# VectorE's own sums in the first slot of three, and the background matmuls off the slots of the groups of 6

## The chip, the cores and the metric

The kernel runs on one core of one Trainium2 chip. The metric is the time of one execution on the device in microseconds (us); less is better. The engines are called PE (TensorE), DVE (VectorE), ACT (ScalarE), POOL (GpSimd) and SP (SyncE, which issues the DMAs), as in the profile.

## The reference

Input is x of shape (8, 128, 36, 36) in float32: 8 images, 128 channels, 1296 positions. Cut to what matters:

```python
x = x + conv_attention(group_norm(x))          # 3x3 convolutions to q, k, v; softmax attention
t = tokens(x)                                  # (8, 1296, 128)
h = layer_norm(t)
q = h @ Wq.T + bq;  k = h @ Wk.T + bk
scores = einsum('bijd,d->bij', tanh(q[:, :, None] + k[:, None]), w) + bw
t = t + softmax(scores) @ h                    # additive attention over all pairs of tokens
t = t + expert_ffn(layer_norm(t))              # 64 experts, each takes the 8 best tokens
```

The third part is by far the largest: for each of 8 x 1296 x 1296 pairs of tokens it wants the sum of 128 values w[d] tanh(q[i,d] + k[j,d]).

## The kernel before, in words

**The loop over pairs.** The tanh's are not computed one by one. Signed sums of groups of 5 or of 6 of the channels give exponentials of queries and keys (qf and kf), and for each group two products over 32 or 64 rows: a numerator n and a denominator d. The score is the sum over all groups of n/d. The division is made by ACT as exp(-ln d), called lq.

A **unit** is one image b (8), one chunk c of 432 queries (3), and one tile j of 128 keys (10, and an eleventh, the "remainder" tile of 16 keys). A full unit has NP = 12 **slots**, numbered k = 0 to 11. They come in triples: k % 3 = 0 and 1 are two slots of the groups of 5 (each with two products on 32 rows, and the rows alternate between the upper and the lower half), k % 3 = 2 is a slot of the groups of 6 (two products on 64 rows). In this text slots 0, 1 and 2 mean the place in a triple. A remainder unit has 2 slots with another layout (`REM_SLOTS`). In all there are 240 full and 24 remainder units.

In slot p of the loop the engines are given, in this order:

1. `take_turns(p, k)`: background steps that move a result out of PSUM (on DVE or ACT);
2. `numerators(p)`: two matmuls n, each into a bank of its own (L949);
3. `denominators(p + LAG)`: two matmuls d for the slot three later (L949), ACT's Ln of them (L972), and in every odd slot the Exp over two slots (L975);
4. `terms(p, ns)`: DVE multiplies n by lq. In most slots the products go into a tile rp (L1003) and POOL adds them up in accp (L1010, L1012). In the slots of `DVE_PAIRS` DVE also adds: it multiplies in place in PSUM (L997) and adds both banks to its own sum accd (L999); in the first of these slots it writes accd at once (L992, then L993, L994);
5. `matmul_turn(p, k)`: matmuls of one background step.

After the last slot of a unit POOL adds the two halves of accp and accd (L1019, L1021), and seven slots later ACT makes e = exp(score) of it (L1032). For a remainder unit matmuls (L1045, rem) add up rp instead.

**Background.** While one image is in the loop, the normalization, convolutions (pc), first attention (s, pa0), tokens and keys (pk) of the next image, the query blocks of the next chunk (pq), the weighting with e (pa1) and the gates of the image before run as generators in four lanes: `first_of_all`, `urgent`, `gates`, `background`. Each generator says whether its next step wants matmuls or takes a result. A slot gives matmuls to one step at most. Only `first_of_all` may run in every slot; the others are kept out of `take_turns` in the slots of `DVE_PAIRS`, and out of `matmul_turn` in the slot just before one of these, or when a balance of columns (`PACE` = 400 more per slot) is below zero:

```python
def take_turns(p, k):
    for lane in lanes:
        if lane.due(p, False) and (k not in DVE_PAIRS or lane is first_of_all):
            lane.run(p)
```

**PSUM.** Of the 8 banks, 4 are two pairs for d (`ps_d`, each pair freed by ACT's Ln), and 4 (`ps_n`) go in turn to n (two a slot) and to every background result (one a step).

**Order.** Nothing is reordered later (`manual_schedule`): each engine runs its instructions in the order in which the loop gives them, and waits where a buffer or an operand isn't there.

Of the kernel before, what the change touches and what calls it, by code (L numbers as in the profile page):

```python
# [54 lines left out]
NP = len(SLOTS)  # L55
IN_TURN = [m + i for m in range(NF // 2) for i in (0, NF // 2)]
LAG = 3
SHIFT = 6.5
DVE_PAIRS = (2, 5, 8, 11)
PACE = 400  # L60


# [8 lines left out]
def kernel(  # L71
# [58 lines left out]
    with ExitStack() as loop, ExitStack() as score:  # L130
# [277 lines left out]
        def conv_keys(b):  # L408
            k = convolved["k"] = big_tile("k0")
            if b == 0:  # L410
                taps["k"] = load_taps("wk_t")
            for r0, nr in KROWS:
                yield from conv_turns(
                    taps["k"], (r0, nr), 1, grid(k[:, r0 * WV : (r0 + nr) * WV], WV), True
                )
# [251 lines left out]
        def keys(b, tiles):  # L667

            xT = prepared[b][1]
            yield matmuls(1)  # L670
            for t in tiles:
                o, n = KT[t]
                first = (b, t) == (0, order[0])
                if first:
                    kf_of[0] = kfp.tile([128, NF, 128], F32, tag="kf", name="kf")
                for q0 in (0, NF // 2):
                    some = slice(q0, q0 + NF // 2)
                    pk = aux("pk1").rearrange("p (q t) -> p q t", t=128)
                    for q in range(NF // 2):
                        bmm(pk[:, q, :n], a_k[:, (q0 + q) * 128 : (q0 + q + 1) * 128],  # L680
                           xT[:, o : o + n], start=True, stop=True)
                    yield TAKE
                    if first:
                        ks = kf_of[0][:, some, :]
                    else:
                        ks = kstp.tile([128, NF // 2, 128], F32, tag="ks", name="ks")
                    nc.scalar.activation(ks[:, :, :n], pk[:, :, :n], AF.Exp)
                    kd3 = kd[b][t].rearrange("p (q t) -> p q t", t=128)[:, some, :]
                    if n == REM:

                        for x in range(2):
                            nc.gpsimd.tensor_scalar(
                                ks[:, :, (x + 1) * n : (x + 2) * n], ks[:, :, :n],
                                pairs[:, min(q0, 1), x : x + 1], None, ALU.mult,
                            )
                        nc.sync.dma_start(kd3[:, :, : 2 * n], ks[:, :, n : 3 * n])
                    else:
                        nc.sync.dma_start(kd3, ks)
                    if q0 > 0:
                        made.add((b, t))  # L700
                    yield matmuls()
# [85 lines left out]
        def gating(b):  # L787
            yield from gate_logits(b, range(NCH))
            yield from gate_tokens(b)
# [114 lines left out]
        def residuals(n):  # L904

            for b in range(n):
                res.append(big_tile("res")[:, :N])
                nc.sync.dma_start(res[b], t2d[b])
                yield step()
# [11 lines left out]
        slots = []  # L921
# [4 lines left out]
        def prefetch(u):  # L926
            if u < len(units) and u not in kf_of:
                b, c, j = units[u]
                assert (b, j) in made
                n = 128 if j < NKT - 1 else 32  # L930
                kf = kfp.tile([128, NF, 128], F32, tag="kf", name="kf")
                nc.sync.dma_start(
                    kf[:, :, :n], kd[b][j].rearrange("p (q t) -> p q t", t=128)[:, :, :n]
                )
                kf_of[u] = kf

        def new_block(b, c, q):
            qf = qfp.tile([128, 2, CH], F32, tag="qf", name="qf")
            qf_of[b, c, q] = qf
            return query_block(b, c, q, qf)  # L940
# [36 lines left out]
        def numerators(p):  # L977
            ns = [ps_n.tile([128, 512], F32, tag="n", name="n") for _ in range(banks(*slots[p]))]
            products(*slots[p], 1, ns)
            return [ps[:, :CH] for ps in ns]  # L980

        def terms(p, ns):

            u, k = slots[p]
            lq = lq_of[u, k // 2]
            o = 2 * (k % 2)
            mult = nc.vector.tensor_mul
            rem = units[u][2] == NKT - 1
            if k in DVE_PAIRS and not rem:
                if k == DVE_PAIRS[0]:  # L990
                    live["d"] = acc.tile([128, CH], F32, tag="accd", name="accd")
                    mult(live["d"], ns[0], lq[:, o, :])  # L992
                    mult(ns[1], ns[1], lq[:, o + 1, :])  # L993
                    nc.vector.tensor_add(live["d"], ns[1], live["d"])  # L994
                else:
                    for h in range(2):
                        mult(ns[h], ns[h], lq[:, o + h, :])  # L997
                    for h in range(2):
                        nc.vector.tensor_add(live["d"], ns[h], live["d"])  # L999
            else:  # L1000
                rp = rpp.tile([128, 2, CH], F32, tag="rp", name="rp")
                for h, n in enumerate(ns):
                    mult(rp[:, h, :], n, lq[:, o + h, :])  # L1003
                if rem:
                    live.setdefault("rem", []).extend(rp[:, h, :] for h in range(len(ns)))
                elif k == 0:
                    live["r"] = rp
                elif k == 1:
                    live["p"] = acc.tile([128, 2, CH], F32, tag="accp", name="accp")
                    nc.gpsimd.tensor_add(live["p"], live["r"], rp)  # L1010
                else:
                    nc.gpsimd.tensor_add(live["p"], live["p"], rp)  # L1012
            if k % 2 == 1:
                lq_of.pop((u, k // 2))
# [53 lines left out]
        balance = [0]  # L1068
# [3 lines left out]
# [5 lines that stand above are left out]
        def matmul_turn(p, k):  # L1077


            before = behind[0]  # L1080
            for lane in lanes:
                while lane.due(p, True) and behind[0] == before:
                    paced = balance[0] < 0 or k + 1 in DVE_PAIRS
                    if lane is not first_of_all and paced or lane is gates and urgent:
                        break
                    lane.run(p)
            balance[0] = min(balance[0] - (behind[0] - before) + PACE, 2 * PACE)
# [25 lines left out]
        for p, (u, k) in enumerate(slots):  # L1113
            b, c, j = units[u]
            rem = j == NKT - 1
            if k == 0:
                prefetch(u + 2)
                if c == 0 and j == 1:
                    if b > 0:
                        gates.append(gating(b - 1))  # L1120
                    if b == NB - 1:
                        gates.append(residuals(4))
                    if b + 1 < NB:
                        background.extend(
                            (normal(b + 1), conv_keys(b + 1), layer0(b + 1), tokens(b + 1),
                             keys(b + 1, range(NKT)))
                        )
            take_turns(p, k)
            ns = numerators(p)
            denominators(p + LAG)  # L1130
            terms(p, ns)
            if pending and pending[0][0] <= p:
                exps(p, *pending.popleft()[1:])
            last = p + 1 == len(slots) or slots[p + 1][0] != u

            if j == order[-1] and u + 1 < len(units) and k % 3:
                used = IN_TURN.index(SLOTS[k][0]) + 1
                if used < NF:
                    first_of_all.append(new_block(*units[u + 1][:2], IN_TURN[used]))
            elif j == order[-2] and last and u + 2 < len(units):  # L1140
                first_of_all.append(new_block(*units[u + 2][:2], IN_TURN[0]))
            matmul_turn(p, k)
            if last and rem:
                first_of_all.append(rem_scores(p, u, live.pop("rem")))
            elif last:
                pending.append((p + 7, u, sums(u)))
        while pending:
            exps(p, *pending.popleft()[1:])
        take_turns(len(slots), 0)
        assert not first_of_all and not gates and not background  # L1150
        score.close()

# [205 lines left out]
```

The softmax here doesn't subtract the row's maximum and nothing guards it: scores larger than these inputs give would overflow.

## Time and profile before

| | |
|---|---|
| median of 3 runs | 6138.88 us (6137.63 to 6139.3) |
| the profiled execution | 6140.74 us |
| its span, first to last instruction | 6139.0 us |
| granted TensorE clock | 0.985 |
| busy: PE, ACT, DVE, POOL | 5957.9, 5279.9, 4796.4, 4597.7 us |
| n matmuls (L949) | 11520 records, 3325.3 us busy |
| d matmuls (L949) | 11520 records, 2991.6 us busy |
| ACT Ln (L972), one | 0.878 us, 2928 times |
| ACT Exp (L975), one | 1.638 us, 1464 times |
| DVE product into rp (L1003), one | 0.600 us, 3912 times |
| DVE product in place (L997), one | 0.608 us, 1440 times |
| DVE sum (L999), one | 0.602 us, 1440 times |
| POOL sum (L1012), one | 2.025 us, 1440 times |

Busy time is the time in which at least one instruction of the engine, or of the group, ran. Each matmul of float32 has two records, so the 11520 records of n are 2 products in 2880 slots. Matmuls on different rows overlap, so the groups of PE add up to more than PE's own busy time. "<-" in brackets names what the instruction, or the weight load before it, had waited for.

### The profile page before, as it was taken

The numbers are of one execution on the slowest core, as the hardware profiler recorded it, in microseconds if no ns is written. First come the engines' busy times: TensorE is split into PE (matmuls) and PEld (weight loads), VectorE is DVE, ScalarE is ACT, GpSimd is POOL, SyncE is SP. The second block draws the span as 40 slices with busy tenths as digits, with TensorE's granted clock in tenths as the row PEclk, the third lists the DMA queues.
The fourth block names the chain that finished last, engine by engine and source line by source line (L and its number), as shares of the span: only waits on it lengthen the run. The fifth ranks groups of instructions, "written<-read, shape, count | busy, mean of one in ns | idle before, by whom it ended". The sixth has DMA issues, their size and how long they took to land.

```text
span 6139.0 us, 93072 instructions
## 1 busy us (share of the span) xinstructions
PE 5957.9 (97%) x33480; PEld 2862.1 (47%) x33480; DVE 4796.4 (78%) x9521; ACT 5279.9 (86%) x5371; POOL 4597.7 (75%) x2819
## 2 busy tenths in 40 slices
PE   7999999999999999999999999999999999999996
PEld 5454444544544445444455444454444544544443
DVE  4787878877788787877888777887778877788882
ACT  1888898888988888889998889888898888999990
POOL 4777777777787777778778786877777777787870
PEclk9999999999999999999999999999999999999997
DMA  1210011100110002100111001110011100110008
GB/s 44 70 37 22 25 62 38 34 25 28 68 43 20 26 27 71 39 24 23 44 55 39 22 24 59 44 39 22 20 65 40 34 25 28 58 50 29 28 20 297
DMA packets 151519, 270.87 MB, mean 44 GB/s; under 512 B 45648, under 2 KB 76752, under 8 KB 151056
## 3 DMA queue, kind: packets, MB, share of 16 engines
q1 hardware_dynamic: 151056, 264.92, 13.0%
q8 instruction: 264, 4.33, 0.3%
q14 instruction: 199, 1.63, 0.1%
HBM read 200.41 MB, written 64.19 MB: 43 GB/s over the span
## 4 chain that ended last, share of the span: by engine, by line
PE 77%; ACT 7%; DVE 6%; issue 6%; POOL 2%; DMA 1%; SPq 0%; DVEq 0%; POOLq 0%; ACTq 0%
PE n L949 37%; PE d L949 12%; PE pa L284 7%; PE pc L284 5%; ACT lq L972 5%; PE s L284 3%; PE pk L284 3%; PE pq L284 3%; DVE rp L1003 2%; DVE n L997 1%; DVE accd L999 1%; PE d L954 1%; ACT lq L975 1%; DMA w<-in_weight_dram 1%; PE n L954 1%
## 5 line engine op out<-in xcount | busy, mean ns | idle before, releaser
L1012 POOL TENSOR_TENSOR accp<-accp,rp 128x864 f32<-128x864 f32 x1440 | 2915.8, 2025 | 1041.0 <-DVE rp L1003 948.8
L949 PE MATMUL n<-qf,kf 32*128 32x432 f32 (+1 forms) x11520 | 3325.3, 574 | 46.5 <-ACT e L1032 13.3
L949 PE MATMUL d<-qf,kf 32*128 32x432 f32 (+1 forms) x11520 | 2991.6, 561 | 38.7 <-ACT lq L972 38.2
L972 ACT ACTIVATE lq<-d 128x864 f32<-128x864 f32 x2928 | 2524.2, 878 | 542.6 <-PE d L949 512.1
L1003 DVE TENSOR_TENSOR rp<-n,lq 128x432 f32<-128x432 f32 x3912 | 2173.3, 600 | 743.5 <-PE d L949 542.8
L975 ACT ACTIVATE lq<-lq 128x1728 f32<-128x1728 f32 (+1 forms) x1464 | 2398.2, 1638 | 46.3
L949 PEld LDWEIGHTS n<-qf,kf 32*128 32x128 f32 (+1 forms) x11520 | 1206.4, 184 | 1600.3 <-DVE rp L1003 581.5
L949 PEld LDWEIGHTS d<-qf,kf 32*128 32x128 f32 (+1 forms) x11520 | 1090.0, 185 | 422.1 <-issue 224.7
L997 DVE TENSOR_TENSOR n<-n,lq 128x432 f32<-128x432 f32 x1440 | 814.9, 608 | 142.1 <-PE n L949 88.5
L999 DVE TENSOR_TENSOR accd<-n,accd 128x432 f32<-128x432 f32 x1440 | 866.3, 602 | 24.6
L1010 POOL TENSOR_TENSOR accp<-rp 128x864 f32<-128x864 f32 x240 | 485.2, 2022 | 197.7 <-DVE rp L1003 195.6
L711 POOL TENSOR_SCALAR qf<-qf,cs_s 128x432 f32<-128x432 f32 x192 | 260.9, 1365 | 45.0 <-ACT qf L710 44.4
L284 PEld LDWEIGHTS pa<-xh,e 128*108 128x108 f32 x1920 | 222.5, 174 | 131.1 <-DVE rp L1003 56.0
L1021 POOL TENSOR_TENSOR accd<-accp,accd 128x432 f32<-128x432 f32 x240 | 265.2, 1105 | 18.8
L1019 POOL TENSOR_TENSOR accp<-accp 128x432 f32<-128x432 f32 x240 | 264.4, 1102 | 16.7
L284 PE MATMUL pa<-xh,e 128*108 128x129 f32 x1920 | 262.9, 283 | 8.7 <-ACT e L1032 5.2
L284 PE MATMUL s<-q,k 128*116 128x432 f32 x480 | 230.3, 568 | 1.7 <-DVE q L316 1.4
L284 PEld LDWEIGHTS pk<-xT,a_k 128*128 128x128 f32 x1408 | 171.2, 192 | 107.0 <-DVE n L997 33.7
L462 POOL TENSOR_TENSOR tot<-tot,e 116x432 f32<-116x432 f32 x192 | 212.0, 1104 | 6.0 <-ACT e L471 4.6
L471 ACT ACTIVATE e<-s 116x432 f32<-116x432 f32 x240 | 124.9, 520 | 98.3 <-PE s L284 97.9
L284 PE MATMUL pa<-e,vw 116*128 116x432 f32 x480 | 204.6, 549 | 0.0
L284 PE MATMUL pk<-xT,a_k 128*128 128x128 f32 (+1 forms) x1408 | 202.5, 287 | 0.1
(213 smaller groups left out, 3788.4 us busy)
## 6 DMA issues: line engine op xcount, KB each, us to landing
kf<-kd SPq DMA_DIRECT2D x239, 512.0 KB
kd<-ks SPq DMA_DIRECT2D x158, 256.0 KB
w<-in_weight_dram SPq DMA_DIRECT2D x32, 1024.0 KB
wk_t<-wk_t_d SPq DMA_DIRECT2D x7, 768.0 KB
wv_t<-wv_t_d SPq DMA_DIRECT2D x7, 768.0 KB
wq_t<-wq_t_d SPq DMA_DIRECT2D x7, 768.0 KB
x<-in_x_dram SPq DMA_DIRECT2D x8, 648.0 KB
t<-tokd SPq DMA_DIRECT2D x96, 54.0 KB
```

The lines of the kernel that those rows point to most:

```text
L284: mm(out, lhsT, rhs, **kw)
L711: nc.gpsimd.tensor_scalar(qf[:, 1, :], qf[:, 0, :], cs_s[:, q : q + 1], None, ALU.mult)
L949: mm(outs[h][:, :CH], kf[rows[h], q, :], qf_of[b, c, q][rows[h], part, :], start=True, stop=True)
L972: nc.scalar.activation(lq[:, o : o + n, :], d[:, :n, :CH], AF.Ln)
L975: nc.scalar.activation(some, some, AF.Exp, scale=-1.0)
L997: mult(ns[h], ns[h], lq[:, o + h, :])
L999: nc.vector.tensor_add(live["d"], ns[h], live["d"])
L1003: mult(rp[:, h, :], n, lq[:, o + h, :])
L1010: nc.gpsimd.tensor_add(live["p"], live["r"], rp)
L1012: nc.gpsimd.tensor_add(live["p"], live["p"], rp)
L1019: nc.gpsimd.tensor_add(s[:, 0, :], s[:, 0, :], s[:, 1, :])
L1021: nc.gpsimd.tensor_add(d, s[:, 0, :], d)
```

## The change

`DVE_PAIRS`, the slots in which DVE adds, goes from k = 2, 5, 8, 11 (the slots of the groups of 6) to k = 0, 3, 6, 9 (the first slot of each triple). The rules that refer to it move along: background results are now taken in slots 1 and 2 of a triple rather than 0 and 1. Background matmuls, kept out of the slot before, are now behind slots 0 and 1 rather than behind slots 2 and 0. A "% NP" makes this rule hold over the end of a unit. The first two rp tiles of a unit are those of k = 1 and 2 rather than 0 and 1. `place` keeps the two slots of a remainder unit as they were: the first may have background matmuls behind it, the second may not, and both may take.

```diff
-DVE_PAIRS = (2, 5, 8, 11)
+DVE_PAIRS = (0, 3, 6, 9)
...
-                elif k == 0:
+                elif k == 1:
                     live["r"] = rp
-                elif k == 1:
+                elif k == 2:
                     live["p"] = acc.tile([128, 2, CH], F32, tag="accp", name="accp")
                     nc.gpsimd.tensor_add(live["p"], live["r"], rp)
...
-                    paced = balance[0] < 0 or k + 1 in DVE_PAIRS
+                    paced = balance[0] < 0 or (k + 1) % NP in DVE_PAIRS
...
-            take_turns(p, k)
+            place = (1, NP - 1)[k] if rem else k
+            take_turns(p, place)
...
-            matmul_turn(p, k)
+            matmul_turn(p, place)
...
-        take_turns(len(slots), 0)
+        take_turns(len(slots), 1)
```

## The prediction

> **What bounds the kernel now.** I read part 1 of the page first, then the chain of waits, the timeline of one stretch, and last the table of waits.
>
> ```profile
> PE 5957.9 (97%) x33480; PEld 2862.1 (47%) x33480; DVE 4796.4 (78%) x9521; ACT 5279.9 (86%) x5371; POOL 4597.7 (75%) x2819
> PE 77%; ACT 7%; DVE 6%; issue 6%; POOL 2%; DMA 1%; SPq 0%; DVEq 0%; POOLq 0%; ACTq 0%
> ```
>
> TensorE (PE) carries 77% of the chain that ended last, but ScalarE (ACT, 86%) is not far behind: where little background work is about, ACT sets the pace. A busy PE is also no proof of work, since a matmul that waits in the middle of a pair shows its neighbour as busy. So I looked at single slots. The timeline at 2016 us shows a whole triple of slots with convolution work (pc) behind slots 0 and 2:
>
> ```profile
> 2016.32 0.63 PE L949 MATMUL n<-qf,kf 32*128 32x432 f32 x2
> 2016.34 0.63 PE L949 MATMUL d<-qf,kf 32*128 32x432 f32 x2
> ...
> 2017.26 1.36 PE L284 MATMUL pc<-xwin,wq_t 128*128 128x216 f32 x6
> 2017.35 1.12 DVE L1003 TENSOR_TENSOR rp<-n,lq 128x432 f32<-128x432 f32 x2 [0.25 <-PE d L949]
> ...
> 2018.55 0.63 PE L949 MATMUL n<-qf,kf 32*128 32x432 f32 x2
> ...
> 2019.49 1.00 PE L949 MATMUL n<-qf,kf 64*128 64x432 f32 x4
> ...
> 2020.32 0.89 PE L949 MATMUL d<-qf,kf 64*128 64x432 f32 x4
> ...
> 2020.72 1.12 DVE L997 TENSOR_TENSOR n<-n,lq 128x432 f32<-128x432 f32 x2
> ...
> 2021.14 1.03 PEld L284 LDWEIGHTS pc<-xwin,wq_t 128*128 128x128 f32 x6 [0.62 <-DVE rp L1003]
> ...
> 2021.75 1.24 DVE L999 TENSOR_TENSOR accd<-n,accd 128x432 f32<-128x432 f32 x2
> ...
> 2022.43 0.19 PEld L949 LDWEIGHTS n<-qf,kf 32*128 32x128 f32 x2 [0.27 <-DVE accd L999]
> ```
>
> The reader is to see three things. In a slot of 5 (32 rows) n and d start together on different rows and both are over in 2017.26 - 2016.32 = 0.94 us. In a slot of 6 (64 rows) d follows n: 2021.14 - 2019.49 = 1.65 us. And VectorE's own sums (L997, L999) stand in the slot of 6; the next n starts just as the first L999 ends. The triple takes 6.11 us.
>
> I measured every slot of the loop in the trace's records, from its first n matmul to that of the next slot: slots 0, 1, 2 of a triple take 1.89, 1.31 and 2.76 us in the mean (5.95 a triple; 960 triples and the 48 slots of the remainder tiles make the loop's 5825 us). The shortest slot with the same work behind it is 0.84 us for a bare slot of 5 and 1.65 for a bare slot of 6; with pc behind 2.14 and 2.85, with s 1.85 and 2.56, with pk 1.93 and 2.74, with pa x4 2.59 and 3.30. Summed over all slots these shortest lengths make 4969 us, so 854 us are waits: 261 in slots 0, 319 in slots 1, 274 in slots 2. The table of waits says on what:
>
> ```profile
> PEld n L949 <- DVE rp L1003: 581.5, 1032, 1.5
> PEld n L949 <- DVE accd L999: 198.5, 472, 1.6
> PEld d L949 <- ACT lq L972: 146.1, 199, 5.0
> ```
>
> (columns: total us, times, longest; about 0.27 us of each is the weight load's usual distance.) n waits for a PSUM bank that VectorE has to free.
>
> **What the Trainium skill says.** *TensorE: Matmul & The Clock Gate*, section "The mechanism", says that matmuls on different row groups overlap while matmuls stay in program order; the trace agrees (four matmuls in 0.94 us at 2016.32). So a blocked n holds up d and the background matmul behind it. *Perfetto Trace Analysis*, "Optimization Strategy", says that the same gap repeating on the engine that should be saturated can mean too few SBUF or PSUM buffers; the L949 waits above fit that.
>
> **The change part by part.** The counts of all instructions stay the same. What moves is which slot VectorE's four-step sums and the background matmuls stand in.
>
> *The rotation of banks.* n and the background results take turns in the four ps_n banks A to D, so every fourth taker gets the same bank. Before, with work behind slots 2 and 0: slot 2 takes B, C, its background D, the next slot 0 takes A, B. That slot's second n needs B, free after the first L999 of slot 2. PE's cover between the two n is 1.65 + background, 2.56 us with s, 2.85 with pc. After, with work behind slots 0 and 1: slot 0 takes A, B, background C, slot 1 takes D, A. Its second n needs A, free after the first L999 of slot 0. The cover is now 0.84 + background: 1.85 with s or pq, 1.93 with pk, 2.14 with pc, 2.59 with pa x4.
>
> *What has to be covered.* From the start of n to the start of the first product is 1.10 us (5th percentile in all kinds of slots; 1.03 in the stretch shown). From there to the end of the first L999 is 1.63 us (5th percentile 1.62, median 1.63 of 720). Sum 2.72; with about 0.06 to the matmul, 2.78. The second n stands 0.11 behind the first. So the stall is 2.78 - 0.11 - cover: 0.82 us with s or pq, 0.74 with pk, 0.53 with pc, 0.08 with pa x4. In the first triple of a unit L992 frees A after one step (1.10 + 0.60), and no stall is left: it applies to three triples in four. With nothing behind slot 0 the wait moves to the next taker of A and is up to 1.1 us, mostly where ACT sets the pace anyway.
>
> *Sum on PE.* 674 of 960 slots 0 have background behind them now; three quarters of these by a mean of 0.5 us over the mix (an estimate from the four stalls above) is **+253 us**. Background behind a slot of 5 costs PE 0.09 us more than behind a slot of 6 (1.85 - 0.84 against 2.56 - 1.65 with s, the same with pc and pa, none with pk); some 640 move: **+55 us**. Queued behind a stalled n are d, and so ACT's Ln of it, and the background matmul.
>
> *What comes back.* The waits of before do not all stay. Slot 2 no longer takes a bank that an eviction issued one slot earlier must free (n needed C one bare slot after background 0; now a slot with background lies between), and stalls give ACT time to catch up. Per unit of 12 slots the floor rises from 20.3 to 20.5, with the stalls 22.8 us, against ACT's 21.6 busy and 23.8 measured now. In 86 of 239 units the new PE path alone is longer than the whole unit now, 95 us in sum; in the rest the stall replaces waits in part. I take back 130 of the 308: **+170 us net**, my choice between 95 and 308. After the remainder tiles the first rp of a unit now comes in slot 1 rather than 0, so that VectorE's wait for rem (1.97 against 1.63 us for such a slot 1, 24 times) goes: -8 us, in the rounding.
>
> *Costed at nothing.* GpSimd's additions: rp is made in slots 1 and 2 rather than 0 and 1, and after the last slot come one addition of 2.02 and two of 1.10 us; e is wanted seven slots (14 us) later. SyncE's DMAs (kd, kf, tokd) move by one slot, and kf is fetched two units (48 us) ahead. Each background step still meets two matmul slots and two eviction slots in three; the pace of 400 a slot is unchanged. Query blocks keep slots 1 and 2. If one of these covers failed, L1012's buffer (rp) would be late next.
>
> The profiled execution is 6140.7 us (span 6139.0), 1.9 above the median 6138.9; from the median, 6139 + 170 = **6310 us**.
>
> **The rivals.**
> *ACT hides it.* Where ACT is at 6.0 of 6.35 us (triples with pk) or 5.7 of 6.2 (s), PE's stall may fall into time that PE waits now. For it: 854 us of waits. Against: with pc ACT has 5.2 of 6.11 and PE runs without pause, so about 126 triples pay 0.3 to 0.4 us whatever happens. Net -50 to +90 us: 6090 to 6230, likely 6180.
> *Faster.* Slots of 2.1, 2.1, 1.65 us on PE are more even than 2.1, 0.9, 2.85, and evictions get a slot more. If all 274 us of waits in slots 2 vanish and the four-step sums are in time, -274 + 55 = -219: 5920. It decides from where 0.84 + background reaches 2.67 us; only pa comes close, so I expect a part of it at most (-30 to -220).
> *d comes in bursts.* d of slot 2 and of the next slot 0 now follow within 1 us, after a gap of up to 3 us; ACT idles in the gap and is late after it. With two d banks this would add 0.2 us to most triples on top: 6310 + 150 = 6460.
> That the code does not do what it says is excluded by the order of instructions of the changed program: L997 stands in slots 3, 6, 9 and pc behind slots 0 and 1.
>
> **How the numbers follow.** Stall as summed, 0.52; hidden by ACT 0.20 (of which faster 0.02, same 0.05, slower 0.13); faster by evenness 0.15; bursts 0.13. Cases of more than 0.2% (12 us, about what a measurement of this kernel can tell from no change): faster 0.17, same 0.05, slower 0.78. The range 6080 to 6470 takes in hidden, summed and bursts; the main case alone is 6200 to 6400.
>
> **What would show it.** "PEld n <- DVE accd L999" grows from 198 us to above 400; slots 1 (or 0 to 1 together) grow by about 0.5 us and slots 2 shrink to near 1.65 to 1.8; "PEld n <- DVE rp L1003" falls; ACT's share falls to about 84%. Wrong if L999 waits do not grow, or if slot 2 loses more than slots 0 and 1 gain.

## The result, and the profile after

The changed kernel takes 6349.24 us (median of 4 runs, 6345.87 to 6351.59) against 6139.09 us for the kernel before: ratio 1.0343, 95% interval 1.033 to 1.0356, so 210 us slower. The profiled execution takes 6351.6 us, its span is 6349.9 us.

Part 1 of the page after (busy us, share of the span) and the engine line of part 4, the chain that ended last:

```profile
PE 6059.6 (95%) x33480; PEld 2874.2 (45%) x33480; DVE 4809.4 (76%) x9521; ACT 5305.9 (84%) x5371; POOL 4599.7 (72%) x2819
PE 82%; DVE 10%; ACT 3%; issue 3%; POOL 2%; DMA 1%; SPq 0%; POOLq 0%; DVEq 0%; ACTq 0%
```

No engine has more to do: the counts are the same, and DVE, ACT and POOL are busy for nearly as long as before. But DVE's part of the chain has gone from 6 to 10%. The table of waits after (who waited for whom: total us, times, longest us):

```profile
PEld n L949 <- DVE rp L1003: 498.3, 924, 2.3
PEld n L949 <- DVE accd L999: 399.4, 627, 2.0
...
PEld d L949 <- ACT lq L972: 119.1, 165, 4.8
...
PE n L949 <- DVE accd L999: 84.9, 170, 1.3
```

The wait of n for the sums (L999) has doubled from 198.5 us, with another 84.9 us put down to the matmul itself; the waits for rp and, for d, for ACT's Ln have become smaller.

The granted TensorE clock makes little of the difference. It is 0.982 in this execution, 0.985 before; between the first and the last slot the trace records half the clock for 137 us, before for 89 us. Even if PE did nothing but compute in these 48 us more, that would be 24 of the 210 us.

The timeline after, of a slot 0 and a slot 1 with background s behind each (start us, us, engine line, operation):

```profile
2004.45 0.73 PE L949 MATMUL n<-qf,kf 32*128 32x432 f32 x2
...
2005.49 0.98 PE L284 MATMUL s<-q,k 128*116 128x432 f32 x2
2005.55 1.13 DVE L997 TENSOR_TENSOR n<-n,lq 128x432 f32<-128x432 f32 x2 [0.53 <-PE d L949]
...
2006.40 1.46 PE L949 MATMUL n<-qf,kf 32*128 32x432 f32 x3
2006.59 1.24 DVE L999 TENSOR_TENSOR accd<-n,accd 128x432 f32<-128x432 f32 x2
...
2007.24 0.18 PEld L949 LDWEIGHTS n<-qf,kf 32*128 32x128 f32 x1 [0.54 <-DVE accd L999]
...
2007.25 0.63 PE L949 MATMUL d<-qf,kf 32*128 32x432 f32 x2
...
2008.17 0.28 PEld L284 LDWEIGHTS s<-q,k 128*116 128x116 f32 x2 [0.62 <-DVE accd L999]
```

n of slot 1 begins at 2006.40, 1.95 us after n of slot 0, and only its first product can run. The second waits until 2007.24, just after the first L999 has ended (two of them take 1.24 us from 2006.59), and d and s wait behind it. Note that PE appears busy through all of this: the row "n x3" of 1.46 us covers the stall. Between n of slot 0 and that second product lie 2.79 us here; the prediction's working has 2.78.

Slot by slot in the records, from the first n to the next slot's: slots 0, 1 and 2 take 1.83, 2.35 and 1.98 us in the mean after, against 1.89, 1.31 and 2.76; 6.16 against 5.95 us a triple. The exact difference of 0.203 us over 960 triples is 195 us; the first slots of the 24 remainder units add 12 us (see below). Of 543 places where slot 0 (3, 6 or 9) has background behind it and a full unit's slot follows, the second n starts 40 to 75 ns after the end of the first L999 in 507.

Before and after by kind of triple (means, us):

| background behind the triple | before | after |
|---|---|---|
| two steps pc | 6.11 | 6.69 |
| two steps pk | 6.35 | 6.32 |
| two steps s | 6.22 | 6.24 |
| pa x4, then s | 6.20 | 6.23 |
| none | 4.75 | 5.16 |

### The profile page after: what moved, and what is told of

Read it like the earlier page. It is cut to its first block, busy times and chain, and to the rows that moved or that the text cites. A ratio compares the mean times of both kernels' runs of the same rounds, so it can differ in the third digit from the quotient of the medians.

```text
span 6349.9 us, 92821 instructions
## 1 busy us (share of the span) xinstructions
PE 6059.6 (95%) x33480; PEld 2874.2 (45%) x33480; DVE 4809.4 (76%) x9521; ACT 5305.9 (84%) x5371; POOL 4599.7 (72%) x2819
## 4 chain that ended last, share of the span: by engine, by line
PE 82%; DVE 10%; ACT 3%; issue 3%; POOL 2%; DMA 1%; SPq 0%; POOLq 0%; DVEq 0%; ACTq 0%
PE n L949 41%; PE d L949 14%; PE pa L284 7%; PE pc L284 5%; DVE n L997 4%; PE s L284 3%; PE pk L284 3%; PE pq L284 3%; DVE accd L999 2%; ACT lq L972 2%; DVE rp L1003 1%; PE n L954 1%; DMA w<-in_weight_dram 1%; PE d L954 1%; POOL accp L1012 1%
## 5 line engine op out<-in xcount | busy, mean ns | idle before, releaser
L949 PE MATMUL n<-qf,kf 32*128 32x432 f32 (+1 forms) x11520 | 3436.0, 575 | 121.1 <-DVE accd L999 84.9
L949 PE MATMUL d<-qf,kf 32*128 32x432 f32 (+1 forms) x11520 | 2947.9, 563 | 37.7 <-ACT lq L972 37.4
L949 PEld LDWEIGHTS n<-qf,kf 32*128 32x128 f32 (+1 forms) x11520 | 1197.8, 185 | 1777.8 <-DVE rp L1003 498.3
L999 DVE TENSOR_TENSOR accd<-n,accd 128x432 f32<-128x432 f32 x1440 | 867.7, 603 | 24.7
L1010 POOL TENSOR_TENSOR accp<-rp 128x864 f32<-128x864 f32 x240 | 486.0, 2025 | 231.5 <-DVE rp L1003 230.7
L992 DVE TENSOR_TENSOR accd<-n,lq 128x432 f32<-128x432 f32 x240 | 145.9, 608 | 192.7 <-PE d L949 182.8
```

The source lines that it names most:

```text
L949: mm(outs[h][:, :CH], kf[rows[h], q, :], qf_of[b, c, q][rows[h], part, :], start=True, stop=True)
```

## The experiments

**What is it: the sums' slot or the background's place?** The first two runs do one half of the change each; `KEPT` takes the place of `DVE_PAIRS` in the two rules for the lanes. The first cut is against the kernel before, the second against the changed kernel.

```diff
-DVE_PAIRS = (2, 5, 8, 11)
+DVE_PAIRS = (0, 3, 6, 9)
+KEPT = (2, 5, 8, 11)     # lanes as before; rp starts at k = 1, 2
```

> VectorE's sums move to slots 0, the background stays behind slots 2 and 0 as before. Theory (the bank that the sums in slot 0 hold is wanted by the second n of slot 1, with a cover of only 0.84 us + background): the stall is there in full and the 55 us for background behind slots of 5 are not, so 6290 to 6350, my value 6310. Rival (where the background stands is what costs): 6139 to 6190.

Measured 6513.54 us, ratio 1.061 (1.0593 to 1.0628). The sums' slot alone does more than the whole change: the theory's direction, but 200 us above its value and outside both ranges. In the records the second n of slot 1 loses 343 us to the sum, nearly what it loses after the whole change (354). What the expectation had missed is the second bank: here slot 1 is bare, so the first n of slot 2 wants the bank of the second sum at once (slots 1 in which the next n starts on a sum's end hold 162 us above their shortest length), and the second n of slot 2 loses a further 131 us to that sum (65 after). The table of waits of this run shows both together (its L1000 is the L999 of the kernel before):

```profile
PEld n L950 <- DVE accd L1000: 738.7, 1042, 3.2
```

So the changed background, behind slot 1, repairs part of what the moved sums do.

```diff
-DVE_PAIRS = (0, 3, 6, 9)
+DVE_PAIRS = (2, 5, 8, 11)
+KEPT = (0, 3, 6, 9)      # lanes as after; rp starts at k = 0, 1
```

> The sums stay in the slots of 6, the background goes behind slots 0 and 1. Theory: the second n of slot 1 waits for a plain product alone, which is early; the bank that L999 frees goes to the background behind the next slot 0, with a cover of 1.65 + 0.84 = 2.49 against 2.78, so a stall of 0.3 us in some 480 triples (up to 140 us), and 55 us for the place: 6180 to 6290, my value 6230. Rival (background placement is what costs): about 6350. Rival (even slots are faster once the sums don't hold the bank): under 6139.

Measured 6230.26 us, ratio 1.0147 (1.0132 to 1.0163), on the value. The waits are those of the theory, too: background now waits more for the bank of a sum. The first two lines are of the kernel before, the others of this run (L1000 is again the sum):

```profile
PEld pa L284 <- DVE accd L999: 35.9, 50, 1.2
PEld pc L284 <- DVE accd L999: 29.4, 47, 0.6
PEld pa L285 <- DVE accd L1000: 126.8, 136, 1.2
PEld pc L285 <- DVE accd L1000: 66.6, 89, 0.9
```

Background off the slots of 6 does not pay while the sums stand there. Against the kernel before, the halves cost 373 and 90 us, but together 210.

**Is it the holding of the bank?** The next run was to free the banks early.

```diff
-                        mult(ns[h], ns[h], lq[:, o + h, :])
+                        mult(dp[:, h, :], ns[h], lq[:, o + h, :])     # dp: an rp tile
...
-                        nc.vector.tensor_add(live["d"], ns[h], live["d"])
+                        nc.vector.tensor_add(live["d"], dp[:, h, :], live["d"])
```

> The changed kernel, but in the slots of the sums VectorE writes the products into an rp tile in SBUF and adds from there, so that a bank is free after its product and not after its sum. Number of steps the same. Theory: the bank is free 1.10 + 0.60 us after n starts, below the cover of 1.85, and the wait of n for L999 goes: 6139 + 55 and less waits elsewhere, 6130 to 6210, my value 6170. Rival (bursts of d, or ACT, set the time): stays above 6300.

Measured 6993.16 us, ratio 1.1388 (1.1371 to 1.1405): both expectations missed. The wait for the sums did go: of the 543 places none has the second n start with the end of a sum. But the sums now read two operands from SBUF and have become nearly twice as long. The group of the sums in the list of costliest groups (busy us, mean ns | idle before), and its durations (minimum, median, maximum in ns):

```profile
L1000 DVE TENSOR_TENSOR accd<-dp,accd 128x432 f32<-128x432 f32 x1440 | 1613.7, 1121 | 24.8
L1000 DVE TENSOR_TENSOR accd<-dp,accd x1440: 596/831/3505, 169.2 to 6835.0; 128x432 f32<-128x432 f32 x180
```

Against 603 ns with a PSUM operand that is 1440 x 0.52 = 746 us more on DVE, and n now waits for rp (956.9 us). The granted clock was lower as well (0.944 against 0.982). The run changed more than the one thing and doesn't decide.

**Dose.** The sums of the changed kernel in the other order:

```diff
-                    for h in range(2):
+                    for h in (1, 0):
                         nc.vector.tensor_add(live["d"], ns[h], live["d"])
```

> The changed kernel with the two sums in the other order, the second bank's first: the first bank is free one step (0.61 us) later, nothing else changes. Theory: the stall grows by 0.6 us in the some 500 triples with background behind slot 0, 300 us less what falls into waits on ACT: 6480 to 6650, my value 6570. Rival (bursts of d, or ACT): within 40 us of 6349.

Measured 6450.37 us, ratio 1.0506 (1.049 to 1.0521): 101 us above the changed kernel. The 300 us were wrong, for a reason that the records give: in 495 of the 543 places the second n again starts 40 to 75 ns after the third step, though that is the *other* bank's sum now. It seems that whichever bank is released first goes to the next taker, so that the order only swapped the two. What did change is the third step itself, which now follows directly on the product that it needs and ends 1.771 instead of 1.636 us after the first product began. That is a dose of 0.135 us in 720 triples, 97 us in all, and 101 came out. But only some 500 of these triples show the stall, which makes 68 us, and the trace records half the clock for 75 us more than in the changed kernel (212 against 137 us of the loop), which can cost up to 38 us. So a later sum does cost time, and about as much as it is late where the stall is; that it is paid for in full in every triple isn't shown.

**Without the sums.** Both kernels with the loop of L999 taken out; they leave out these products' share of the scores:

```diff
-                    for h in range(2):
-                        nc.vector.tensor_add(live["d"], ns[h], live["d"])
```

> The changed kernel without the two sums L999 in slots 3, 6 and 9: it leaves out these products' share of the scores; matmuls, products and the order of all else stay. A bank is then free after its product. Theory: all of the wait of n for L999 (354 us in slots 1, 65 in slots 2) goes, VectorE is also relieved: 6110 to 6190, my value 6150. Rival (the place of the background or bursts of d cost): above 6280.

> The kernel before without its two sums in slots 5, 8 and 11, the same work left out as in the run beside it. Theory: only the 80 + 31 us of waits for L999 and some of those for rp go: 6040 to 6110, my value 6080, and the kernel with the changed slots stays 30 to 110 us (55 by the working) above it, the price of background behind slots of 5. Rival: a difference near the 210 us of the change itself.

Measured 6031.98 us (ratio 0.9819, 0.9802 to 0.9835) with the changed slots and 6059.21 us (0.9862, 0.9847 to 0.9877) with the slots of before. The 210 us are gone, and the sign has turned: the changed place of the background is 27 us faster when no sum holds a bank. So the sums cost 6349 - 6032 = 317 us in slots 0 and 6141 - 6059 = 82 us in the slots of 6; the difference, 235, less 27, is the change's 208. Of my 55 us for background behind slots of 5 the shortest slot lengths show 24 (they add up to 4923 against 4899 us), and the waits above them are lower by 55 (788 against 843). In this pair VectorE is relieved too, by the same 1440 steps on both sides, so it is the difference that counts. The pair shows that the place of the sums makes the 210 us. That they do it by holding banks, and not by delaying VectorE's steps behind them, is read from the records of the changed kernel: 507 of 543 second n start right after a first sum, while the waits of n for the plain products (rp), which such a delay would lengthen, fell from 581.5 to 498.3 us.

**Can the sums be made to hold less?** Product and sum by turns, in both kernels:

```diff
                     for h in range(2):
                         mult(ns[h], ns[h], lq[:, o + h, :])
-                    for h in range(2):
                         nc.vector.tensor_add(live["d"], ns[h], live["d"])
```

> The changed kernel with product, sum, product, sum rather than two products and two sums: the first bank is free some 0.38 us earlier, the second some 0.15 us later. Theory: with background behind slots 0 and 1 the second n takes the first bank and the background behind slot 1 at once wants the second, so the wait only moves from n to that background: 6290 to 6370, my value 6330. Rival (only the first bank counts, as the 101 us for 0.135 us in the run with the other order suggest): 0.38 x 506 = 190 us less, near 6160.

> The kernel before with product, sum, product, sum. Its second bank is wanted only 1.65 + background + 0.84 us later, so the later freeing of it is covered, and the 206 waits for L999 in slots 0 (80 us) go in part: 6060 to 6130, my value 6090. Rival (the longer chain of dependent steps delays VectorE): 6140 to 6200.

In the changed kernel 6355.67 us, ratio 1.0345 (1.033 to 1.0361): no gain, as the theory said. The second n of slot 1 loses about 200 us to the sums instead of 354, but that of slot 2 120 instead of 65, and the mean slot 2 grows from 1.98 to 2.09 us. Background waits longer for a sum, too (L998 is the sum; in the changed kernel it is 26.9 and 21.9 us). So the wait moved to the next takers:

```profile
PEld pc L284 <- DVE accd L998: 78.5, 94, 0.9
PEld pa L284 <- DVE accd L998: 61.1, 78, 0.9
```

In the kernel before 6142.36 us, ratio 1.0001 (0.9992 to 1.0009): the gain of 50 us that I expected isn't there. The waits for the sums in slots 0 fell from 80 to 29 us, but all waits of n for the sums together rose from 198.5 to 240.8. The later sum is not covered, as I had thought: in slots 1 the first n starts right after it in 84 places, before in 10.

**Spreading the sums.** VectorE sums only the second product, but in two slots of three; the first product goes to rp and GpSimd. `HALF_SLOTS` holds the two places in a triple.

```diff
+                own = k % 3 in HALF_SLOTS
+                mult(rp[:, 0, :], ns[0], lq[:, o, :])
...
+                elif own and k > 1:
+                    mult(ns[1], ns[1], lq[:, o + 1, :])
+                    nc.vector.tensor_add(live["d"], ns[1], live["d"])
+                    nc.gpsimd.tensor_add(live["p"][:, 0, :], live["p"][:, 0, :], rp[:, 0, :])
```

> The changed background (behind slots 0 and 1), but VectorE's sums spread: in slots 0 and 1 it sums the second product alone, and the first goes to rp and to GpSimd as half an addition (1.10 us); in slot 2 both go to GpSimd. Steps per unit: VectorE 30 against 31, GpSimd 18.0 us against 18.4. No sum holds the first bank, and the second is free after three steps (2.72 us) and wanted after 0.84 + background + 0.84, 2.7 us at the least. Theory (the holding of the banks is the whole price): near the 6032 us without sums, 6040 to 6110, my value 6070, faster than both kernels. Rival (VectorE's and GpSimd's load, or twice as many chained sums, cost): above 6140.

> The same with the sums in slots 0 and 2 (VectorE 31 steps, GpSimd 18.1 us). Slot 2 is where an eviction stands ahead of the sums and PE gives the shortest cover in time (1.65 us with nothing behind it), so VectorE is later there: 6060 to 6140, my value 6090, above the run beside it. Rival: the same as that within 15 us.

> The background as before (behind slots 2 and 0), sums of the second product in slots 0 and 2. Theory: the 82 us that the sums cost there (6141 against 6059) go in part, 6060 to 6130, my value 6095, and the changed background is then the faster one by 0 to 40 us. Rival (the place of the background costs 55 us once the banks are free): this one is the fastest.

Measured 6350.78 us (1.0343, 1.0326 to 1.036), 6279.11 us (1.0225, 1.0209 to 1.024) and 6293.08 us (1.0246, 1.0231 to 1.0262). All three missed by 190 to 280 us. The waits of the first of them:

```profile
DVE rp L998 <- PE d L950: 592.1, 774, 12.2
PEld n L950 <- DVE rp L998: 471.2, 728, 3.4
...
PEld n L950 <- DVE accd L1005: 227.9, 372, 1.2
DVE rp L998 <- POOL accp L1010: 190.4, 107, 3.6
```

The waits for sums fell (227.9 against 399.4), but every slot now needs an rp tile, and a tile is free only when GpSimd has added it up: DVE waits 190.4 us for GpSimd (L1010; 8.1 us in the changed kernel). GpSimd has entered the chain that ended last, with 15% against 2% in the changed kernel (11 and 10% in the other two runs):

```profile
PE 61%; POOL 15%; DVE 9%; issue 8%; ACT 6%; DMA 1%; POOLq 0%; SPq 0%; DVEq 0%; ACTq 0%
```

The expectation had a wrong sum here. It set GpSimd at 18.0 us a unit against 18.4, but the changed kernel makes seven additions of 2.02 us and two of 1.10, which is 16.4. So GpSimd got more to do, not less: it is busy for 4989.2 us against 4599.7. Besides, product and sum of one bank depend on each other in twice as many slots, and the granted clock was lower in the two runs with the changed background (0.969 and 0.968, against 0.982 after). How much each of these costs is open; the runs show only that this split is no way out. No version tried that does all the work beats the kernel before.

## Why the prediction was right, point by point

- **6310 was forecast, 6349 came**, by the mechanism of the likeliest case: the second n of slot 1 waits for the first L999 of slot 0. From n of slot 0 to that second n the working has 2.78 us; where it starts after the sum, the median is 2.72: 1.03 to the first product (1.10 was set), 1.64 to the end of the first L999, and 0.055 to the matmul.
- **The signs.** The wait on the weight load reached 399.4 us, at the edge of the "above 400", with 84.9 more on the matmul; the wait for rp fell, and ACT's share is 84%, as forecast. Slots 0 and 1 together grew by 0.98 us, twice the 0.5 that was set, since work moved there from slots 2; and slots 2 shrank only to 1.98, not to 1.65 to 1.8.
- **The size of the stall** was 253 us from 505 triples at 0.5 us. The records show 354 us from 506 starts at 0.70 us. For the kinds of background with a worked-out stall the rule was right: some 275 starts behind pc, s, pq, pk or pa x4 stall by 0.59 us in the mean, and the four figures give 0.58 for them. The other 230 or so, behind transposes, other sizes of pa and the like, stall by 0.80 us; for these nothing was worked out, and the mean over the mix was set too low. That the second n follows the first after 7 ns when nothing holds it, not 0.11 us, and that the product starts at 1.03 and not 1.10, nearly cancel.
- **The net is in part luck.** The working adds 253 + 55 = 308 us and takes 130 back. In the records the sums hold the second n of slots 1 and 2 for 354 + 65 us, and before they held slots 0 and 1 for 80 + 31: again 308 us more, of which 100 came back. But the items differ: the stall was 101 us larger, the 65 us were put at nothing, the 55 us weren't there, and the 111 us stood under what comes back. Errors of both signs left 39 us.
- **The 55 us for background behind slots of 5** are wrong as a net price. Without the sums the place gains 27 us. The faster rival, more even slots, may have this small part of the truth; what makes the gain no run shows.
- **What comes back** was set at 130 us of 308. Of the old waits for sums 111 us (80 in slots 0, 31 in slots 1) went, and in slots 2 the wait for rp fell from 134 to 74 us. The 22.8 us for a unit with stalls do not follow from the sum: 253 us over 240 units add 1.05 to the 20.5, which makes 21.6. The 86 units and the 95 us, if they rest on it, are off with it.
- **"ACT hides it"** fits one sort of triple: those with pk or s gained or lost no more than 0.03 us, as their ACT load (6.0 and 5.7 us) suggested. No run changed that load, so the reason isn't shown. Those with pc paid 0.58 us, more than the 0.3 to 0.4 foreseen; ACT had 5.3 us in them. Triples without background paid 0.41 us, though I had put their wait down to time in which ACT sets the pace anyway.
- **The rotation** was told too simply: it seems that banks don't go strictly in turn, and that the one released first goes to the next taker. For the kernels before and after the two readings agree; the run with the other order of sums shows the difference.
- **One line was read too far.** At 2022.43 of the stretch before, n starts 0.09 us after the first L999 ends, but it doesn't wait for it: the 0.27 us before its weight load is the usual distance, the same as at 2018.55. PE runs without pause there, as the prediction's own rival says.
- **Bursts of d**: the wait of d for ACT's Ln fell from 146.1 to 119.1 us, and without the sums the same order of d takes 6032 us. This rival is out.
- **The remainder tiles** were to give 8 us. VectorE's wait for rem went, but the slot 1 after a remainder unit grew from 1.97 to 2.07 us, and the first remainder slot from 2.78 to 3.30, since more background now stands behind it. The slot between them fell from 1.60 to 1.43: about +11 us in all in 24 units.

## What to carry to other kernels

A chain of steps that works in place in PSUM holds its banks until its last reader. What counted here is how much other work the matmul engine has between the product that fills the bank and the next taker of a bank. Count that cover in time for each place where the chain could stand, and for every kind of work that can stand in between, not for the commonest ones alone. In this kernel the chain did best behind the longest matmuls, even though that looks less even. Bringing the first freeing forward and putting the second back only moved the wait on.

## What the runs showed of the hardware that I had not expected

- A VectorE sum of 128x432 floats took 607 ns (median) with both inputs in SBUF while GpSimd was idle (some 550 instructions), but 1499 ns when a GpSimd instruction ran for between half and 95% of it (551), up to 3505 ns. GpSimd's own sums hardly changed (2.04 us in the mean, 2.03 in the changed kernel). With one input in PSUM the VectorE sum took 603 ns in the mean in the changed kernel, beside much the same GpSimd load. The Trainium skill's page *VectorE: DVE Perf Modes*, section "Two Vector instructions with no wait between them", names the second SBUF read interface as shared with GpSimd; the run agrees in that VectorE slows down while GpSimd works.
- A VectorE step that needs the result of the step just before it took longer than one that doesn't: two products and a sum took 1.636 us in the changed kernel, where the sum followed the other product, and 1.771 us in the run with the other order, where it followed its own.
